# Storing a layer's result per image in 2-KB pieces, and turning it into rows in SBUF, in a four-layer kernel whose order a planner sets

## The chip, the core and the metric

The kernel runs on one core of a Trainium2 chip, everything in float32. The metric is device time in microseconds (us), the median of repeated runs. The engines are PE (matmul; PEld are its weight loads), DVE (vector), ACT (scalar), POOL (GpSimd) and SP, which here only issues DMAs. DMAs are issued by SP, ACT and POOL, and each issuing engine has a DMA queue of its own in the profile: q1 is SP's, q10 ACT's, q0 POOL's.

## What is computed

Four layers on x of shape [8 images, 384 channels, 32, 32]:

```
x = L0(x)   # rmsnorm; Mamba forward and backward: h = dA*h + dBu per channel and 16 states; 3x3 depthwise gate; residual
x = L1(x)   # 1x1, 3x3 depthwise, 1x1; linear attention over the 1024 pixels; layernorm; MLP 384-1536-384, gelu; residuals
x = L2(x)   # one 13x13 depthwise convolution and six smaller ones, each with batch norm, summed
x = L3(x)   # 1x1 + residual, 13x13 depthwise convolution and a scaled identity, gelu
```

Layers 2 and 3 each come down to one 13x13 depthwise convolution with merged taps; in the kernel they are convolution a and convolution b.

## The kernel before

**Layers 0 and 1** (`_layers01`) work image by image. `front(b)` does layer 0's dense part, `scan(b)` the recurrence, `layer1(b)` all of layer 1. Their instructions are woven: while `scan(b)` goes through its 48 steps (12 units of 128 channels and half an image, 4 steps of 4 states each; one `yield` a step), a list of jobs (lines 1195 to 1222) advances `front(b+1)` and `layer1(b-1)` in proportion. `layer1(7)` has no scan beside it and runs alone at the end. A function can be put off by some steps with `defer`, and `tick` calls what is due.

In a scan step ACT computes `da` (L847, the exponentials, four buffers), DVE `du` (L852) and two scans `hs` (L864), POOL multiplies `hs` (L873), and PE adds up states into `acc` (L558). The inputs `dlt`, `vr` and `bct` come by SP's queue (L793, L779). When the backward half of a unit is complete, DVE makes `zr` and POOL stores it to `g_d` (L821). `layer1` begins by loading `g` back (L952, SP) and multiplying it by a weight (`op`, L540), which DVE adds to `xx` (L959).

**Layer 1's result x2** goes to DRAM in `x2_d`, laid out as [channel, image row, RL]: a row holds the 8 images side by side, 32 columns each with 6 zeros before it (`PADW`), RL = 313 in all. `fold` first fills all of `x2_d` with zeros (three DMAs of 5 MB, L901, POOL). `last(h, acc)` adds the MLP's output to `xx` (L1140) and stores it (L1143, POOL), three DMAs for each half image: for every channel 16 pieces of 128 B, one per row of the image.

**Convolution a** (`conv`) takes 8 channels at a time. `load` brings their rows into 32 partitions, one per image row (L301, POOL: 256 pieces of 1252 B); `shift` (L307, DVE) makes three copies that are shifted by one, two and three columns; a group of 4 channels then is 16 matmuls on each of four column groups of PE (L331). The moving operand is 8 images of 32 columns, found by a step of 38 elements in the row. Tap windows come by SP and ACT (L246). The result goes to `y2_d`, the 1x1 of layer 3 (L377) makes `xp_d`, laid out as `x2_d` was, and convolution b reads that.

SBUF tiles of a kind rotate through a fixed number of buffers: `a6` (6 KB a partition) has 7, for `xx`, `g`, `hh`, `dw`, `ln`, `xn` and others. The pool of convolution a reuses the space of the layers before it, each tile waiting for what lay there.

**The order** on each engine is not the program's: `Plan` simulates the program with estimates of every instruction (`Step`, `Engines`) and adds edges that fix the order so found. The engines run in order, so an instruction that waits holds up all that stand behind it on its engine, DMA issues included.

Of the kernel before, what the change touches and what calls it, by code (L numbers as in the profile page):

```python
# [17 lines left out]
P = 128  # L18
C = 384
# [24 lines left out]
AHEAD = 5000  # L44
TP = H * KT
PADW = KS // 2
HIMG = H // 2 * (W + 2)
UL = L + 6
# [21 lines left out]
def tile_layers(  # L70
# [38 lines left out]

    RL = PADW + B * (W + PADW) + 3  # L110
    x2_d = dram.tile([C, H, RL], FP, tag="x2_d", name="x2_d")
    y2_d = dram.tile([C, H, B, W], FP, tag="y2_d", name="y2_d")
# [118 lines left out]

    NB_C = C // NCH
    wins = {}
# [20 lines left out]
    _layers01(tc, nc, B, xv, x2_d, dram, ident, mean_w, eps5, eps6, one, half, minus1, vec, bns, bnt,  # L254
              rs, rsm, inproj_t, xproj_t, dtproj_t, outproj_t, taps1, taps3, taps3b, sel, alog,
# [3 lines left out]
    NQ = C // 4  # L259
    GB = 4  # L260
    with tc.tile_pool(name="cx", bufs=2, reuse_waits="tile") as cxp, tc.tile_pool(
        name="cps", bufs=6, space=PSUM, reuse_waits="tile"
# [12 lines left out]
        for q in range(4):  # L275
            nc.scalar.dma_start(gbias[q * H : (q + 1) * H, :], biasq_d[q, :].partition_broadcast(H))
        def conv(g_d, src_d, tag, put, far):

            xts = {}

            def places(n):

                return [H * ((n % 2 * 2 + e) % NSH) for e in range(NSH)]

            def load(n):
                for m in range(n, min(n + 1 + N_WIN // 2, NB_C)):
                    if (tag, m) not in wins:
                        load_windows(g_d, tag, m, [nc.sync, nc.scalar])  # L290
                if n >= NB_C:
                    return
                at = places(n)
                if "pool" in more and n % 7 >= 4:
                    xt = more["pool"].tile([P, NCH, RL], FP, tag="xu", name=f"xt_{tag}_{n}")
                else:
                    xt = cxp.tile([P, NCH, RL], FP, tag="xt", name=f"xt_{tag}_{n}", bufs=4)
                src = bass.AP(
                    src_d.tensor, src_d[NCH * n, 0, 0].offset, [[RL, H], [H * RL, NCH], [1, RL]],
                )  # L300
                nc.gpsimd.dma_start(xt[at[0] : at[0] + H], src)  # L301
                xts[n] = xt

            def shift(n):
                at, xt = places(n), xts[n]
                for e in (1, 2):
                    nc.vector.tensor_copy(  # L307
                        xt[at[e] : at[e] + e * H, :, 0 : RL - e - (e - 1)],
                        xt[at[0] : at[0] + e * H, :, e : RL - (e - 1)],
                    )  # L310


            for n in range(far):
                load(n)
            shift(0)
            for g in range(NQ):
                n, first = divmod(4 * g, NCH)
                if first == 0:
                    load(n + far)
                    if n + 1 < NB_C:  # L320
                        shift(n + 1)
                    xt, tp = xts.pop(n), wins[tag, n]
                ps = cps.tile([P, HALF], FP, tag="cv", name=f"cv_{tag}_{g}")
                for t in range(KT):
                    for e in range(4):
                        c = first + e
                        row = xt[:, c, NSH * t : NSH * t + B * (W + PADW) - PADW]
                        rhs = bass.AP(
                            row.tensor, row.offset, [row.ap[0], [W + PADW, B], [1, W]]
                        )  # L330
                        nc.tensor.matmul(  # L331
                            ps[H * e : H * (e + 1), 0:BW],
                            tp[:, c, :].rearrange("p (j t) -> p j t", t=KT)[:, :, t], rhs,
                            start=(t == 0), stop=(t == KT - 1), skip_group_check=True,
                        )
                put(g, ps[:, 0:BW])
# [13 lines left out]

        conv(g2_d, x2_d, "a", put2, 2)

# [52 lines left out]
        with tc.tile_pool(name="xu", bufs=3, reuse_waits="tile") as more["pool"]:  # L405
            conv(g3_d, xp_d, "b", put3, 5)


def _layers01(tc, nc, B, xv, x2_d, dram, ident, mean_w, eps5, eps6, one, half, minus1, vec, bns, bnt,
              rs, rsm, inproj_t, xproj_t, dtproj_t, outproj_t, taps1, taps3, taps3b, sel, alog,  # L410
# [11 lines left out]
    with ExitStack() as ctx:  # L422
# [29 lines left out]
        vv = v_d.rearrange("b d (c p) l -> b d p c l", p=P)  # L452
        x2v = x2_d.rearrange("(c p) h r -> c p h r", p=P)

# [442 lines left out]
        def fold():  # L897

            RL = x2_d.shape[2]
            for c in range(NC):  # L900
                fill = nc.gpsimd.dma_start(  # L901
                    x2v[c], zero[:, 0:RL].rearrange("p (o r) -> p o r", o=1).to_broadcast([P, H, RL])
                )

                tc.add_manual_dep(fill.ins, newest[0].ins.name, behind, reason="fill")
                yield 2
            for c in range(NC):
# [36 lines left out]
        def layer1(b):  # L944
# [190 lines left out]
            behind_gelu = []  # L1135

            def last(h, acc):
                for m in range(NC):
                    o = xx[h][:, m, :]
                    nc.vector.scalar_tensor_tensor(  # L1140
                        o, acc[m], vec("mlp_b2", m), o, ALU.add, ALU.add
                    )
                    nc.gpsimd.dma_start(  # L1143
                        x2v[
                            m, :, h * (H // 2) : (h + 1) * (H // 2),
                            PADW + b * (W + PADW) : PADW + b * (W + PADW) + W,
                        ],
                        rows(o),
                    )

# [107 lines left out]
class Step:  # L1258
    def __init__(self, ins, kind_of):
# [16 lines left out]
        elif self.dma:  # L1276
            total = 4 * _count(self.outs[0][1])
            piece = min(4 * _run(self.outs[0][1]), 4 * _run(self.ins[0][1]), 8192)
            self.work = total / piece * (12 + 0.05 * piece) / 16
            self.ns = {"SP": 52.0, "Activation": 330.0, "Pool": 500.0 + min(2048, total / piece) * 0.33}[self.engine]  # L1280
        elif self.engine == "Activation":
# [17 lines left out]
class Engines:  # L1299
    def __init__(self):  # L1300
        self.free = dict.fromkeys(ENGINES, 0.0)
        self.cells, self.mode, self.last = {}, None, 0.0
        self.table, self.port, self.queue = 1, 0.0, 0.0
        self.window, self.busy, self.half = 0, {}, set()

    def clock(self, t):
        now = int(t // CLOCK_NS)
        while self.window < now:
            if self.busy.pop(self.window, 0.0) < BUSY_SHARE * CLOCK_NS:
                self.half.add(self.window + 1)  # L1310
            self.window += 1
# [8 lines left out]
    def put(self, s, ready):  # L1320
        e = s.engine
        if e == "PE":
            t = max(ready, self.free[e])
            if s.mode != self.mode:
                t = max(t, self.last + (95 if self.mode else 0))
                self.cells, self.mode = {}, s.mode
# [24 lines left out]
        if s.table and s.table != self.table:  # L1351
            t, self.table = t + 1290, s.table
        self.free[e] = t + s.ns
# [13 lines left out]
class Plan:  # L1367
    def __init__(self, nc, tiles, traced, spans, bias):
# [30 lines left out]
        self.users = users  # L1399
        areas = {}  # L1400
        for name, t, _, space, size, lo, tag in spans:
            if name in users and kind_of[name] in ("SB", "PSUM"):
                pool = re.sub(r"^.*_(\w+_\d+)$", r"\1", tag)
                areas.setdefault(kind_of[name], []).append((t, lo, lo + max(1, size // P), name, pool))
        for entries in areas.values():
            entries.sort()
            whole = {}
            for _, lo, hi, _, pool in entries:
                a, b = whole.get(pool, (lo, hi))
                whole[pool] = (min(a, lo), max(b, hi))  # L1410
            held, opened = [], {}
            for _, lo, hi, name, pool in entries:
                if pool not in opened:
                    a, b = whole[pool]
                    opened[pool] = sorted({x[2] for x in held if x[0] < b and a < x[1]})
                gates = sorted({x[2] for x in held if x[0] < hi and lo < x[1]}) + opened[pool]
                rest = []
# [5 lines left out]
                held = rest + [(lo, hi, name)]  # L1423
                for g in gates:
                    self.freed.setdefault(g, []).extend(users[name])
# [216 lines left out]
```

## Time and profile before

| | |
|---|---|
| median of 3 runs | 4902.2 us (4898.8 to 4903.2) |
| profiled execution, own time | 4989.3 us |
| its span | 4987.5 us |
| granted PE clock, mean | 0.902 |
| PE busy | 4260.8 us (85%) |
| DVE busy | 3806.8 us (76%) |
| ACT busy | 2712.1 us (54%) |
| POOL busy | 2857.9 us (57%) |
| DMA | 965.3 MB, 194 GB/s |

The stages, from the starts of their instructions: scan 0 begins at 149.8 us, scans 1 to 7 at 657, 1139, 1633, 2136, 2627, 3122 and 3611, each some 490 us; layer 1 of the last image alone from 4046 to 4398; convolution a from 4425 to some 4625; the 1x1 to 4770; convolution b to the end. In the profile's lines `x_d<-xx` is the store of x2, `x_d<-zero` the fill, `x_d<-xr` a store of layer 0, `g_d<-zr` the store of g and `xt_a<-x_d` convolution a's row load (buffer and tensor numbers are left out of names). A line gives the start, the busy time, the engine, the source line, the operation, and in brackets the engine's idle time before it and what ended that.

### The profile page before, as it was taken

How to read it: one execution, taken by the hardware profiler on the slowest of the kernel's cores; microseconds unless marked ns; L12 is line 12 of the kernel's file. 1: busy time of each engine (PE TensorE's matmuls, PEld its weight loads, DVE VectorE, ACT ScalarE, POOL GpSimd, SP SyncE). 2: the span in 40 equal slices, each digit the busy share in tenths (PEclk: the TensorE clock that was granted, in tenths of full speed). 3: DMA queues.
4: the chain of work that ended last, by engine and by line, in shares of the span. 5: the costliest groups of instructions: out<-in, count | busy, mean ns of one | idle time of the engine just before them, and what ended most of it. 6: DMA issues, size and time to landing. Idle time of an engine off the chain costs nothing. (4 is left out here: it accounts for less than half of the span.)

```text
span 4987.5 us, 58465 instructions
## 1 busy us (share of the span) xinstructions
PE 4260.8 (85%) x20128; PEld 1764.7 (35%) x20128; DVE 3806.8 (76%) x3861; ACT 2712.1 (54%) x3786; POOL 2857.9 (57%) x1546
## 2 busy tenths in 40 slices
PE   6665689889989898899888999899988969978888
PEld 2121123333333333333333333333333324457457
DVE  1789989988888898888988998798889840147366
ACT  2546456775587568756875677568645722100212
POOL 1456666666666665666566666565766660024069
PEclk9676699899989998999999989998988978989999
DMA  8985566478747874787478757875763673379788
GB/s 210 277 268 186 191 211 221 158 204 210 225 163 209 209 229 161 202 209 229 167 206 213 227 170 205 214 228 171 171 191 126 165 151 84 63 137 258 224 210 188
DMA packets 543121, 965.29 MB, mean 194 GB/s; under 512 B 56568, under 2 KB 220904, under 8 KB 542824
## 3 DMA queue, kind: packets, MB, share of 16 engines
q1 hardware_dynamic: 401648, 663.89, 45.8%
q0 software_dynamic: 58048, 205.76, 16.5%
q10 hardware_dynamic: 83128, 91.90, 7.0%
q8 instruction: 159, 2.61, 0.2%
q14 instruction: 138, 1.13, 0.1%
HBM read 726.36 MB, written 234.98 MB: 193 GB/s over the span
## 5 line engine op out<-in xcount | busy, mean ns | idle before, releaser
L873 POOL TENSOR_TENSOR hs<-hs,bct 128x1024 f32<-128x1024 f32 x768 | 2260.3, 2944 | 984.3 <-DVE carry L869 517.8
L847 ACT ACTIVATE da<-dlt,neg_a 128x512 f32<-128x512 f32 x1536 | 1026.7, 714 | 697.6 <-DVE hs L864 621.2
L852 DVE TENSOR_TENSOR du<-vr,bct 128x1024 f32<-128x1024 f32 x768 | 1052.9, 1371 | 45.3 <-DMA vr<-v_d 27.6
L864 DVE TENSOR_TENSOR_SCAN hs<-da,carry,du 128x512 f32<-128x512 f32 x768 | 946.7, 1267 | 96.1 <-PE acc L558 61.0
L864 DVE TENSOR_TENSOR_SCAN hs<-da,du 128x512 f32<-128x512 f32 x768 | 904.1, 1209 | 65.8 <-ACT da L847 19.9
L558 PE MATMUL acc<-hs,selt 128*32 128x512 f32 x2304 | 610.6, 672 | 102.5 <-POOL hs L873 102.5
L540 PE MATMUL mf<-ln,w 128*128 128x512 f32 x1152 | 552.1, 621 | 48.3 <-DMA w<-w_d 18.0
L1173 PE MATMUL mo<-hm,w 128*128 128x512 f32 x1152 | 526.9, 596 | 0.0
L553 PE MATMUL acc<-hs,selt 128*32 128x512 f32 x768 | 444.9, 676 | 89.1 <-POOL hs L873 63.0
L847 ACT ACT_TABLE_LOAD x282 | 361.8, 1283 | 10.3 <-DMA bct<-bc_d 2.0
L540 PEld LDWEIGHTS mf<-ln,w 128*128 128x128 f32 x1152 | 217.3, 197 | 360.0 <-issue 284.8
L1173 PEld LDWEIGHTS mo<-hm,w 128*128 128x128 f32 x1152 | 215.0, 190 | 291.9 <-issue 282.6
L540 PE MATMUL in<-xn,win 128*128 128x512 f32 x576 | 281.8, 626 | 9.9 <-ACT uz L669 5.2
L331 PE MATMUL cv_a<-xt_a,tp_a 128*32 128x256 f32 x3072 | 181.9, 388 | 48.8 <-DMA xt_a<-x_d 27.8
L1143 POOL DMA_DIRECT2D x_d<-xx x48 | 56.6, 1181 | 276.8 <-DVE xx L1140 275.9
L540 PE MATMUL op<-g,wo 128*128 128x512 f32 x288 | 149.9, 671 | 75.8 <-DMA g<-g_d 75.1
L331 PE MATMUL cv_b<-xt_b,tp_b 128*32 128x256 f32 x3072 | 180.2, 392 | 27.6 <-DVE xt_b L307 15.5
L558 PE MATMUL dw<-dw_i,t3b 96*32 96x512 f32 x1056 | 194.1, 641 | 6.5 <-DMA dw_i<-h_d 6.1
L553 PEld LDWEIGHTS acc<-hs,selt 128*32 128x32 f32 x768 | 63.4, 115 | 365.2 <-issue 241.7
L307 DVE COPY xt_b<-xt_b 32x2496 f32<-32x2496 f32 (+1 forms) x96 | 151.8, 1581 | 49.8 <-DMA xt_b<-xp_d 47.3
L331 PEld LDWEIGHTS cv_a<-xt_a,tp_a 128*32 128x32 f32 x3072 | 157.1, 138 | 73.9 <-DVE xt_a L307 28.7
L558 PEld LDWEIGHTS acc<-hs,selt 128*32 128x32 f32 x2304 | 91.9, 114 | 235.5 <-POOL hs L873 166.2
(196 smaller groups left out, 5891.2 us busy)
## 6 DMA issues: line engine op xcount, KB each, us to landing
dlt<-dl_d SPq DMA_DIRECT2D x384, 256.0 KB, 4.2
vr<-v_d SPq DMA_DIRECT2D x384, 256.0 KB, 5.0
bct<-bc_d SPq DMA_DIRECT2D x256, 256.0 KB, 5.4
ut<-u_d SPq DMA_DIRECT2D x192, 257.5 KB, 4.9
lc_i<-xn_d SPq DMA_DIRECT2D x192, 228.8 KB, 4.9
dw_i<-h_d SPq DMA_DIRECT2D x192, 228.8 KB, 6.2
w<-w_d SPq DMA_DIRECT2D x64, 576.0 KB, 5.2
w<-in_w SPq DMA_DIRECT2D x64, 576.0 KB, 6.4
```

The source lines that it names most:

```text
L307: nc.vector.tensor_copy(xt[at[e] : at[e] + e * H, :, 0 : RL - e - (e - 1)], xt[at[0] : at[0] + e * H, :, e : RL - (e - 1)],)
L331: nc.tensor.matmul(ps[H * e : H * (e + 1), 0:BW], tp[:, c, :].rearrange("p (j t) -> p j t", t=KT)[:, :, t], rhs, start=(t == 0), stop=(t = ...
L540: product = nc.tensor.matmul(ps, w[:, k, m * P : (m + 1) * P], rhs[k] if isinstance(rhs, list) else rhs[:, k, :], start=(k == 0), stop=(k ...
L553: first = product()
L558: tc.keep_in_program_order(product())
L847: nc.scalar.activation(da[:, bass.ts(j, HALF)], dlt[:, bass.ts(j, HALF)], AF.Exp, scale=neg_a[:, g, r : r + 1],)
L852: nc.vector.tensor_mul(pairs(du), pairs(vt), bct[r][:, 0:1, :].to_broadcast([P, 2, HALF]),)
L864: nc.vector.tensor_tensor_scan(t[:, s][:, way], da[:, s][:, way], du[:, s][:, way], k_c if second else 0.0, ALU.mult, ALU.add,)
L873: made.append(nc.gpsimd.tensor_mul(pairs(t), pairs(t), bct[r][:, 1:2, :].to_broadcast([P, 2, HALF])))
L1143: nc.gpsimd.dma_start(x2v[m, :, h * (H // 2) : (h + 1) * (H // 2), PADW + b * (W + PADW) : PADW + b * (W + PADW) + W,], rows(o),)
L1173: nc.tensor.matmul(acc[m], wb[:, f, m * P : (m + 1) * P], hm, start=(i == 0 and f == 0), stop=(i == FF // C - 1 and f == NC - 1),)
```

## The change

x2 is stored in its natural order in a new tensor `x2i_d` [image, channel, pixel], so that a piece is 512 pixels of a channel, 2 KB. For images 0 to 6 a new step `turn` reads it back with one partition per image row and stores whole padded rows into a new `x2_d`; there is no fill any more. Image 7 isn't turned: convolution a reads it from `x2i_d` directly. `load` for convolution a becomes one POOL load (images 0 to 6), two memsets of pads and one SP load (image 7), and a row of the tile now holds images outermost and 8 channels inside. Convolution b is as before. The planner's estimates are changed, so the order of all engines is new.

```diff
-    x2_d = dram.tile([C, H, RL], FP, tag="x2_d", name="x2_d")
+    x2_d = dram.tile([NB_C, H, B - 1, NCH, WP], FP, tag="x2_d", name="x2_d")
+    x2i_d = dram.tile([B, C, L], FP, tag="x2i_d", name="x2i_d")
...
+                if last_d is not None:
+                    own = flat(xt)[at[0] : at[0] + H]
+                    near = (B - 1) * NCH * WP
+                    nc.gpsimd.dma_start(own[:, 0:near], src_d[n].rearrange("h b c w -> h (b c w)"))
+                    end = own[:, near : near + (NCH + 1) * WP].rearrange("p (c w) -> p c w", w=WP)
+                    nc.gpsimd.memset(end[:, :, 0:PADW], 0.0)
+                    nc.gpsimd.memset(own[:, XF - 3 : XF], 0.0)
+                    nc.sync.dma_start(
+                        end[:, 0:NCH, PADW:WP],
+                        last_d[NCH * n : NCH * (n + 1)].rearrange("c (h w) -> h c w", w=W),
+                    )
...
-            for c in range(NC):
-                fill = nc.gpsimd.dma_start(
-                    x2v[c], zero[:, 0:RL].rearrange("p (o r) -> p o r", o=1).to_broadcast([P, H, RL])
-                )
...
+            def turn(b, k):
+                t = a6(f"turn_{b}_{k}").rearrange("p c n -> p (c n)")[:, 0 : RC * WP]
+                t = t.rearrange("p (c w) -> p c w", w=WP)
+                nc.gpsimd.memset(t[:, :, 0:PADW], 0.0)
+                for q in range(4):
+                    src = bass.AP(
+                        x2i_d.tensor, x2i_d[b, q * QC + k * RC, 0].offset, [[W, H], [L, RC], [1, W]]
+                    )
+                    nc.sync.dma_start(t[q * H : (q + 1) * H, :, PADW:WP], src)
+                for q in range(4):
+                    n = (q * QC + k * RC) // NCH
+                    nc.scalar.dma_start(
+                        x2_d[n : n + RC // NCH, :, b].rearrange("n h c w -> h n (c w)"),
+                        t[q * H : (q + 1) * H].rearrange("p (n c) w -> p n (c w)", c=NCH),
+                    )
...
-                    nc.gpsimd.dma_start(
-                        x2v[
-                            m, :, h * (H // 2) : (h + 1) * (H // 2),
-                            PADW + b * (W + PADW) : PADW + b * (W + PADW) + W,
-                        ],
-                        rows(o),
-                    )
+                    nc.gpsimd.dma_start(x2v[b][:, m, bass.ts(h, HALF)], o)
+                if h and b < B - 1:
+                    for k in range(QC // RC):
+                        defer(2 * k + 1, partial(turn, b, k))
...
-CLOCK_NS, BUSY_SHARE = 3413.0, 0.8
-LANES = 8
+CLOCK_NS, STAYS, RETURNS = 3413.0, 0.41, 0.83
+LANES, LANDS = 8, 1500
...
+                need = RETURNS if self.window in self.half else STAYS
+                if self.busy.pop(self.window, 0.0) < need * CLOCK_NS:
...
-                t = max(t, self.last + (95 if self.mode else 0))
+                t = max(t, self.last + (0 if not self.mode else 195 if self.mode[1] == "32" else 95))
...
-            self.queue = max(t + 1300, self.queue) + s.work
-            return t, self.queue + 700
+            own = self.queues.get(e, 0.0)
+            if s.small:
+                self.queues[e] = max(t + 1300, own, self.queue - s.work / 2) + s.work
+                self.queue = max(t + 1300, self.queue) + 0.6 * s.work
+            else:
+                self.queues[e] = max(t + 1300, self.queue, own) + s.work
+                self.queue = max(t + 1300, self.queue) + s.work
+            return t, self.queues[e] + LANDS
```

Here C is 384, H and W 32, L 1024, NCH 8, PADW 6, WP 38, QC 96 and RC 32, so `turn` runs three times per image (k = 0, 1, 2). What the planner treats as small DMA writes are those of pieces under 512 B and over 1500 pieces; a switch to another table on ACT is taken at 1400 instead of 1290 ns; and the rule by which tiles of a pool wait for the pools before it is written anew.

More of the change, by code (lines that the diff above doesn't have):

```diff
@@ L45 @@
 TP = H * KT
+NB_C = C // NCH
 PADW = KS // 2
+WP = W + PADW
+QC = C // 4
+RC = 32
 HIMG = H // 2 * (W + 2)
@@ L230, in kernels @@
         yield 1
-    NB_C = C // NCH
     wins = {}
@@ L252, in windows @@
             yield
-    _layers01(tc, nc, B, xv, x2_d, dram, ident, mean_w, eps5, eps6, one, half, minus1, vec, bns, bnt,
+    _layers01(tc, nc, B, xv, x2_d, x2i_d, dram, ident, mean_w, eps5, eps6, one, half, minus1, vec, bns, bnt,
               rs, rsm, inproj_t, xproj_t, dtproj_t, outproj_t, taps1, taps3, taps3b, sel, alog,
@@ L260, in tile_layers @@
     GB = 4
+    XF = B * NCH * WP + WP - W + 3
     with tc.tile_pool(name="cx", bufs=2, reuse_waits="tile") as cxp, tc.tile_pool(
@@ L276, in tile_layers, with conv, flat @@
             nc.scalar.dma_start(gbias[q * H : (q + 1) * H, :], biasq_d[q, :].partition_broadcast(H))
-        def conv(g_d, src_d, tag, put, far):
+        def conv(g_d, src_d, last_d, tag, put, far):
             xts = {}
+            def flat(xt):
+                return xt.rearrange("p c r -> p (c r)")
             def places(n):
@@ L297, in load @@
                     xt = cxp.tile([P, NCH, RL], FP, tag="xt", name=f"xt_{tag}_{n}", bufs=4)
+                if last_d is not None:
[9 more added lines that the diff above has]
+                    )
+                    xts[n] = xt
+                    return
                 src = bass.AP(
@@ L305, in shift @@
                 at, xt = places(n), xts[n]
+                if last_d is not None:
+                    xt = flat(xt)
+                    for e in (1, 2):
+                        nc.vector.tensor_copy(
+                            xt[at[e] : at[e] + e * H, 0 : XF - e - (e - 1)],
+                            xt[at[0] : at[0] + e * H, e : XF - (e - 1)],
+                        )
+                    return
                 for e in (1, 2):
@@ L326, in conv @@
                         c = first + e
-                        row = xt[:, c, NSH * t : NSH * t + B * (W + PADW) - PADW]
-                        rhs = bass.AP(
-                            row.tensor, row.offset, [row.ap[0], [W + PADW, B], [1, W]]
-                        )
+                        if last_d is not None:
+                            row = flat(xt)[:, c * WP + NSH * t : XF]
+                            step = NCH * WP
+                        else:
+                            row = xt[:, c, NSH * t : NSH * t + B * WP - PADW]
+                            step = WP
+                        rhs = bass.AP(row.tensor, row.offset, [row.ap[0], [step, B], [1, W]])
                         nc.tensor.matmul(
@@ L349, in put2 @@
                 nc.gpsimd.dma_start(y2v[g - GB + 1 : g + 1].rearrange("g p n -> p g n"), hold["t"])
-        conv(g2_d, x2_d, "a", put2, 2)
+        conv(g2_d, x2_d, x2i_d[B - 1], "a", put2, 2)
         pbias = cwp.tile([P, NC, 1], FP, tag="pbias", name="pbias")
@@ L405, in tile_layers, with _layers01 @@
         with tc.tile_pool(name="xu", bufs=3, reuse_waits="tile") as more["pool"]:
-            conv(g3_d, xp_d, "b", put3, 5)
-def _layers01(tc, nc, B, xv, x2_d, dram, ident, mean_w, eps5, eps6, one, half, minus1, vec, bns, bnt,
+            conv(g3_d, xp_d, None, "b", put3, 5)
+def _layers01(tc, nc, B, xv, x2_d, x2i_d, dram, ident, mean_w, eps5, eps6, one, half, minus1, vec, bns, bnt,
               rs, rsm, inproj_t, xproj_t, dtproj_t, outproj_t, taps1, taps3, taps3b, sel, alog,
@@ L452, in _layers01 @@
         vv = v_d.rearrange("b d (c p) l -> b d p c l", p=P)
-        x2v = x2_d.rearrange("(c p) h r -> c p h r", p=P)
+        x2v = chunks(x2i_d)
         def const(ap, shape, tag):
@@ L897, in fold @@
         def fold():
-            RL = x2_d.shape[2]
-            for c in range(NC):
-                fill = nc.gpsimd.dma_start(
-                    x2v[c], zero[:, 0:RL].rearrange("p (o r) -> p o r", o=1).to_broadcast([P, H, RL])
-                )
-                tc.add_manual_dep(fill.ins, newest[0].ins.name, behind, reason="fill")
-                yield 2
             for c in range(NC):
@@ L1135, in layer1 @@
             behind_gelu = []
+            def turn(b, k):
[12 more added lines that the diff above has]
+                        t[q * H : (q + 1) * H].rearrange("p (n c) w -> p n (c w)", c=NCH),
+                    )
             def last(h, acc):
@@ L1142, in last @@
                     )
-                    nc.gpsimd.dma_start(
-                        x2v[
-                            m, :, h * (H // 2) : (h + 1) * (H // 2),
-                            PADW + b * (W + PADW) : PADW + b * (W + PADW) + W,
-                        ],
-                        rows(o),
-                    )
+                    nc.gpsimd.dma_start(x2v[b][:, m, bass.ts(h, HALF)], o)
+                if h and b < B - 1:
+                    for k in range(QC // RC):
+                        defer(2 * k + 1, partial(turn, b, k))
             for h in range(2):
@@ L1279, in __init__ @@
             self.work = total / piece * (12 + 0.05 * piece) / 16
+            self.small = piece < 512 and total / piece > 1500 and kind_of.get(self.outs[0][0]) != "SB"
+            if self.small:
+                self.work = total / piece * 60 / 16
             self.ns = {"SP": 52.0, "Activation": 330.0, "Pool": 500.0 + min(2048, total / piece) * 0.33}[self.engine]
@@ L1302, in __init__ @@
         self.cells, self.mode, self.last = {}, None, 0.0
-        self.table, self.port, self.queue = 1, 0.0, 0.0
+        self.table, self.port, self.queue, self.queues = 1, 0.0, 0.0, {}
         self.window, self.busy, self.half = 0, {}, set()
@@ L1308, in clock @@
         while self.window < now:
-            if self.busy.pop(self.window, 0.0) < BUSY_SHARE * CLOCK_NS:
+            need = RETURNS if self.window in self.half else STAYS
+            if self.busy.pop(self.window, 0.0) < need * CLOCK_NS:
                 self.half.add(self.window + 1)
@@ L1342, in put @@
             self.free[e] = t + s.ns
-            self.queue = max(t + 1300, self.queue) + s.work
-            return t, self.queue + 700
+            own = self.queues.get(e, 0.0)
+            if s.small:
+                self.queues[e] = max(t + 1300, own, self.queue - s.work / 2) + s.work
+                self.queue = max(t + 1300, self.queue) + 0.6 * s.work
+            else:
+                self.queues[e] = max(t + 1300, self.queue, own) + s.work
+                self.queue = max(t + 1300, self.queue) + s.work
+            return t, self.queues[e] + LANDS
         if s.lock:
@@ L1351, in put @@
         if s.table and s.table != self.table:
-            t, self.table = t + 1290, s.table
+            t, self.table = t + 1400, s.table
         self.free[e] = t + s.ns
@@ L1399, in __init__ @@
         self.users = users
-        areas = {}
+        areas, turns = {}, {}
         for name, t, _, space, size, lo, tag in spans:
@@ L1404, in __init__ @@
                 areas.setdefault(kind_of[name], []).append((t, lo, lo + max(1, size // P), name, pool))
+                first, final = turns.get(pool, (n, 0))
+                turns[pool] = (min(first, users[name][0]), max(final, users[name][-1]))
         for entries in areas.values():
             entries.sort()
[L1407 to L1411, printed above, removed]
+            members = {}
+            for e in entries:
+                members.setdefault(e[4], []).append(e[3])
+            held = []
             for _, lo, hi, name, pool in entries:
[L1413 to L1416, printed above, removed]
+                gates = {x[2] for x in held if x[0] < hi and lo < x[1]}
+                for other, names in members.items():
+                    if turns[other][1] < turns[pool][0]:
+                        gates.update(names)
                 rest = []
@@ L1423, in __init__ @@
                 held = rest + [(lo, hi, name)]
-                for g in gates:
+                for g in sorted(gates):
                     self.freed.setdefault(g, []).extend(users[name])
```

## The prediction

> **What bounds the kernel now.** I read the page first (span 4987.5 us), then the windows of each image's scan, then the waits, then timelines at the three places where this change acts. The eight scans of layer 0 (one per image, with the previous image's layer 1 and the next image's front woven in) take most of the span. A middle one, its last 28 us before the next image settles, and a hole in the first scan:
>
> ```profile
> 2136.00:2624.00 488.00, 440.62 (x1685) 164.51 (x1682) 421.19 (x419) 331.77 (x452) 303.73 (x146) 0.94 0.70 202
> 1632.20:1660.00 27.80, 23.46 (x81) 8.59 (x79) 26.25 (x31) 9.50 (x15) 17.57 (x14) 0.99 1.02 127
> 250.00:276.00 26.00, 1.92 (x4) 0.18 (x4) 11.64 (x14) 0.02 (x1) 5.20 (x3) 0.50 1.00 269
> ```
>
> Columns: stretch, its length, busy us (instructions) of PE, weight loads, DVE, ACT, POOL, then granted clock, DMA share, GB/s. In 488 us PE works 441 and DVE 421: both are near their limit, DMA (0.70) is not. But right after a scan's end (second line) DMA is full at only 127 GB/s, and in the first scan (third line) everything stands but DMA. What waits on that:
>
> ```profile
> PE op L540 <- DMA g<-g_d: 75.1, 7, 15.0
> POOL hh L578 <- DMA x_d<-xx: 44.2, 5, 12.7
> ```
>
> Seven waits of PE for the load of g (total, times, longest), five of POOL for x2 stores. The timeline after scan 2 shows how:
>
> ```profile
> 1632.20 3.52 POOL L1143 DMA_DIRECT2D x_d<-xx  x3
> 1642.82 0.61 POOL L821 DMA_DIRECT2D g_d<-zr  x1
> 1658.30 0.47 POOL L578 MEMSET hh<- 128x48 f32 x4 [5.45 <-DMA x_d<-xx]
> 1659.70 0.38 SPq L952 DMA_DIRECT2D g<-g_d  x1
> 1665.27 10.08 PE L540 MATMUL op<-g,wo 128*128 128x512 f32 x18 [9.61 <-DMA g<-g_d]
> 1670.23 0.75 DVE L959 SCALAR_TENSOR_TENSOR xx<-op,rsm,xx 128x512 f32<-128x512 f32 x1 [8.92 <-PE op L540]
> ```
>
> POOL issues three x2 stores in 128-B pieces; the small store of g follows on POOL's queue and lands 16.9 us after its issue began. After scan 0, where no x2 store is ahead of it, it took 3.1 us. So the g load starts at 1659.7, PE idles 9.6 us and DVE 8.9 us behind it. The last transition, from layer 1 to convolution a:
>
> ```profile
> 4395.71 2.47 DVE L1140 SCALAR_TENSOR_TENSOR xx<-mo,pk,xx 128x512 f32<-128x512 f32 x3 [59.29 <-PE mo L1173]
> 4400.48 4.89 POOL L271 MEMSET xo<- 128x1878 f32 x3
> 4408.49 1.20 POOL L301 DMA_DIRECT2D xt_a<-x_d  x2 [3.13 <-DMA x_d<-xx]
> 4420.75 8.86 DVE L307 COPY xt_a<-xt_a 32x2496 f32<-32x2496 f32 x6 [22.57 <-DMA xt_a<-x_d]
> 4425.21 15.09 PE L331 MATMUL cv_a<-xt_a,tp_a 128*32 128x256 f32 x220 [27.82 <-DMA xt_a<-x_d]
> ```
>
> PE stands 27.8 us: store landing 11 us, row load 12.3 us, two shifts. Median landings of the stores concerned:
>
> ```profile
> x_d<-zero POOLq DMA_DIRECT2D x3, 5008.0 KB, 45.5
> x_d<-xx POOLq DMA_DIRECT2D x48, 256.0 KB, 16.9
> x_d<-xr POOLq DMA_DIRECT2D x48, 256.0 KB, 5.1
> ```
>
> The third, a store of layer 0 with the same 256 KB in 2-KB pieces, is the form that the x2 store gets.
>
> **The fill (removed).** Three zero fills of 5 MB leave POOL's queue at 170, 190 and 219 us, 45.5 us each. A store behind them (c_d, 237 us) lands 33.2 us after its issue; POOL waits 24.1 us for it, SP and ACT stand behind, and DVE idles 14.8 us at 276.8 (plus 2.6 and 1.2 us on loads). Without the fill that store should land in about 3 us, like its twin at 308 us. Scan 0 is DVE's (462 busy of 506 us), so this idle time is span. Ends: 5 us (another wait comes up) and 19 us. I take **15 us**.
>
> **The x2 store in 2-KB pieces.** POOL's issue falls from 1.18 to 0.58 us (L688): 48 x 0.6 = 29 us of a POOL that is busy 304 of 488, off the path. What counts is landing, 5 instead of 17 us. After scans 1 to 6 DVE's wait at L959 is 12.6, 9.5, 13.2, 11.4, 9.7 and 5.2 us, together 61.6; after scan 0, without x2 stores ahead, it is 2.9. If g lands as there, 61.6 - 6 x 2.9 = 44 us go. Left next is that 2.9 us. The POOL waits of 44 us (L578) mostly overlap those stalls; I count nothing for them. The 15.0-us wait for g after scan 7 has no x2 store in front and stays.
>
> **The turn (added, 7 images x 3).** Each k adds a memset, 4 loads (SP) of 1024 pieces of 128 B, and 4 stores (ACT) of 128 pieces of 1216 B.
> - POOL: 21 memsets of 192 columns; the nearest row (L578, 48 columns) is 0.21 us, so 0.2 to 0.9 each, under POOL's idle time: 0. Uncovered, at most 19 us.
> - SP: 84 issues of 0.5 to 0.7 us, as L793. If the first load is placed before its x2 store has landed, SP stands, and the scan's dlt, vr and bct loads with it; they run ahead by 6 buffers. ACT: 84 issues of 0.33 us, 28 us of an engine 332/488 busy. Its stores wait for the turn's loads, and the exponentials (L847) queue behind; four da tiles cover them, some 4 x 3.7 us of DVE work (two scans of 1.2 and du of 1.2 us). Price 0 while the wait is under that.
> - DMA time. Between 4405 and 4435 us the trace's DMA packets of the x2 stores (32 pieces of 128 B each) took 1067 ns on average, 33 ns a piece. Reads of 128 B into SBUF occur in the trace only as 512 start-up packets: median 13 ns, mean 18. The skill's page "DMA: Bandwidth & Descriptors", section Specifications, speaks against the change: below 512 B an engine does read-modify-write[...]. By that rule the pieces merely move: 12,288 per image x 33 / 16 = 25 us, as before, on SP's queue, and the stalls remain. By the trace's reads it is 12,288 x 13 to 18 / 16 = 10 to 14 us, plus row stores (55 ns, the 1276-B packets) 1536 x 55 / 16 = 5 us. I take the trace's reads: they go the same way (HBM to SBUF), while the 33 ns were measured on writes into HBM. Of the two I lean to the 18 ns, since the turn's pieces lie scattered.
> - Where it lies: in program order 1, 3 and 5 scan steps of some 10 us (490 us / 48) after the last x2 store. The g load comes back some 15 to 25 us after it, so on SP's queue it can stand behind the four loads of k = 0, 0.8 to 1.1 us of DMA each: 0 to 4.4 us. I take 1.5 us for each of six: **-9 us**; ends 0 and -44 (by the rule above, all of the gain).
> - Three more tiles in the 7 a6 buffers may delay hh or xn tiles: in the range only.
>
> Together 44 - 9 = **35 us**.
>
> **Transition and convolution a.** New chain: last DVE result 4396.8 to 4398.2, issue 0.6, landing 3 to 5 (4402), direct load of 256 pieces 3 to 4 (4406), two shifts 3 us, matmul near 4410 instead of 4425.2. If POOL runs the three xo memsets (4.9 us) before the row load, 4412. That is 13 to 18 us; **15 us**. Within convolution a PE has 166 busy of 187 us: row loads carry 272 KB in 8.5-KB runs and 32 KB in 128-B pieces instead of 313 KB; at the rows above 0.7 to 1.9 + 0.2 to 0.5 us of DMA per tile against 2: even. 96 POOL memsets (0.1 to 0.2 us, POOL 72 of 187 busy), SP's 48 loads, the moving rows' step of 304 instead of 38 elements (no row shows it; runs stay 32 long): 0, ends -8 and +5.
>
> **The other order.** The planner's estimates of clock, mode switch, landing and pool gates change, so every queue is reordered. PE idles some 47 us and DVE 67 of a scan's 488, of which the above touches about 10. No row says what the new order gains: between -40 and +100 us over seven scans; I take 0, since waits of the same engines must still be filled.
>
> **Sum.** The profiled execution took 4989.3 us (span 4987.5). 15 + 35 + 15 = 65 gives 4924. The median of the runs is 4902.2, 0.9825 of it: 65 x 0.9825 = 64, so **4838 us**.
>
> **Rivals.**
> 1. The turn takes the stalls' place: its reads cost 33 ns, hold SP's queue, g still comes late. For: DMA is already full there. Against: only SP's ring is shared, and POOL's g store is then free. Leaves 15 + 15 = 30, x 0.98: 4873.
> 2. The order fills idle time too: 10 us more in each of seven scans; 4838 - 69 = 4769. For: 47 us idle; against: no row.
> 3. Slower: ACT stands at the turn's stores. In the crowded stretch loads landed in 15.3 us (dlt, 1645); four in a row plus this could outlast the 15 us of da cover. It decides at 65 / 21 = 3 us uncovered per turn; at 6 us, 126 - 65 = 61 us more, x 0.98: 4962. Against: ACT waits 71 us per scan for DVE, and the planner places the stores after a later landing (1500 instead of 700 ns).
> 4. No change: the boundary stalls return as waits for hs or a6 buffers, and only part of the rest comes: about 4900.
>
> Chances: forecast 0.46 (4815 to 4860), rival 1 0.22, rival 2 0.20, no change 0.05, slower 0.07. A measurement of this kernel can tell about 0.2% from no change. Faster 0.88, same 0.05, slower 0.07. The range 4762 to 4890 leaves out the lower third of rival 2, no change and slower.
>
> **What would show it.** Right: the g store lands in 3 to 6 us after scans 1 to 6 and L959 waits under 5 us; no 15-us DVE gap near 277 us; PE idle before convolution a 10 to 15 us; x2 landing near 5 us. Wrong: turn loads landing over 10 us with g behind them; ACT's exponentials waiting for turn loads; DVE busy per scan unchanged and the idle time grown elsewhere.

## The result, and the profile after

The changed kernel took 4826.4 us (median of 4 runs, 4812.3 to 4835.0) against 4902.7 us for the kernel before beside it: ratio 0.984, 95% interval 0.981 to 0.987, that is 76 us faster (64 were predicted). The kernel before is not equally fast in every set of runs (a set is one group of runs on one chip, with the kernel before among them): it gave 4902.7 here and 4960.2, 4926.4 and 4927.4 us beside the experiments, the first two of these three on the same chip, while the changed one gave 4826.4, 4832.3 and 4835.4. So the ratio itself ranges from 0.975 to 0.984, and the experiments are judged by ratios within their own set and by stage lengths; where the two disagree, both are given. The profiled execution of after took 4812.3 us (span 4810.4), the fastest of its runs; that of before was 87 us over its median. Their difference, 177 us, is therefore not the change's worth.

The windows of the same four places, with the columns as before (stretch, length, busy us of PE, weight loads, DVE, ACT, POOL, clock, DMA share, GB/s): a middle scan, the 28 us behind the end of scan 2, the former hole in scan 0, and convolution a.

```profile
2044.80:2512.50 467.70, 437.10 (x1698) 164.47 (x1697) 432.75 (x424) 335.89 (x455) 310.56 (x152) 0.97 0.71 222
1575.50:1603.30 27.80, 23.90 (x83) 8.17 (x83) 26.57 (x31) 11.20 (x18) 19.48 (x11) 0.94 0.97 258
250.00:276.00 26.00, 16.90 (x90) 4.87 (x82) 25.87 (x34) 9.41 (x15) 15.11 (x6) 0.79 0.87 234
4226.50:4454.50 228.00, 183.35 (x3073) 158.33 (x3073) 151.81 (x141) 17.50 (x47) 87.47 (x155) 0.97 1.07 222
```

The middle scan has become 20 us shorter with nearly the same work of PE (437 us, 441 before); what went is mostly idle time. After the scan's end DMA is nearly as full as before, but moves 258 instead of 127 GB/s. The hole is gone (DVE 25.9 of 26 us). Convolution a, 202.9 us before, is now 228. Its row of before:

```profile
4425.20:4628.10 202.90, 181.91 (x3073) 157.23 (x3073) 154.27 (x141) 17.54 (x47) 76.05 (x67) 0.99 1.07 246
```

PE's work is the same within 2 us; DMA is full in both, but carries less. PE's wait for g, in after's list of waits (total, times, longest):

```profile
PE op L573 <- DMA g<-g_d: 23.3, 3, 17.0
```

75.1 us in seven waits became 23.3 in three, and 17.0 of that is the wait after scan 7, which was expected to stay. DVE's waits for `op` from scan 1 to the end of scan 7, before and after:

```profile
DVE xx L959 <- PE op L540: 61.6, 12, 12.3
```

```profile
DVE xx L984 <- PE op L573: 10.1, 11, 2.6
```

The timeline after scan 2, to be laid beside that of before:

```profile
1575.48 1.66 POOL L1185 DMA_DIRECT2D x2i_d<-xx  x3
1584.75 0.58 POOL L854 DMA_DIRECT2D g_d<-zr  x1
...
1579.90 9.62 SPq L1171 DMA_DIRECT2D turn<-x2i_d  x8
1594.78 0.67 SPq L977 DMA_DIRECT2D g<-g_d  x1
...
1604.55 2.08 PE L573 MATMUL op<-g,wo 128*128 128x512 f32 x2
```

The g store lands 3.6 us after its issue (16.9 before). The g load starts only 6 us after that landing, behind eight loads of the turn and others on SP's queue, yet PE has no gap: the new order gives PE and DVE other work until 1604. After scans 1 to 6 the g store lands in 3.2 to 6.5 us. The transition to convolution a:

```profile
4208.27 2.47 DVE L1182 SCALAR_TENSOR_TENSOR xx<-mo,pk,xx 128x512 f32<-128x512 f32 x3 [54.18 <-PE mo L1212]
...
4213.71 4.86 POOL L276 MEMSET xo<- 128x1878 f32 x3 [2.14 <-DMA xt_a<-x2i_d]
4218.53 0.52 POOL L310 DMA_DIRECT2D xt_a<-x_d  x1
...
4222.08 8.70 DVE L331 COPY xt_a<-xt_a 32x2440 f32<-32x2440 f32 x6 [11.34 <-DMA xt_a<-x_d]
...
4226.51 4.08 PE L364 MATMUL cv_a<-xt_a,tp_a 128*32 128x256 f32 x36 [16.57 <-DVE xt_a L331]
```

PE stands 16.6 us (27.8 before). What ends it is not image 7's direct read but the row load of images 0 to 6, which stands on POOL behind the three memsets of 4.9 us. Median landings:

```profile
x_d<-turn ACTq DMA_DIRECT2D x84, 152.0 KB, 3.6
g_d<-zr POOLq DMA_DIRECT2D x48, 256.0 KB, 2.9
x2i_d<-xx POOLq DMA_DIRECT2D x48, 256.0 KB, 4.6
turn<-x2i_d SPq DMA_DIRECT2D x84, 128.0 KB, 4.9
```

At the median the x2 store lands in 4.6 us, where it took 16.9.

### The profile page after: what moved, and what is told of

Same layout as the page of the kernel before. It is cut to its first block, busy times and chain, and to the rows that moved or that the text cites. A ratio compares the mean times of both kernels' runs of the same rounds, so it can differ in the third digit from the quotient of the medians.

```text
span 4810.4 us, 59001 instructions
## 1 busy us (share of the span) xinstructions
PE 4201.2 (87%) x20128; PEld 1741.9 (36%) x20128; DVE 3834.4 (80%) x3861; ACT 2717.4 (56%) x3788; POOL 2860.2 (59%) x1660
## 4 chain that ended last, share of the span: by engine, by line
PE 45%; DVE 20%; issue 14%; DMA 12%; ACT 6%; POOL 3%; SPq 0%; ACTq 0%; DVEq 0%; POOLq 0%
DVE hs L897 11%; DVE du L885 5%; PE mo L1212 5%; PE mf L573 5%; PE in L573 4%; PE acc L586 4%; DMA tp_a<-g_d 3%; PE kv_kp L1037 2%; PE c L573 2%; PE pj L573 2%; PE kv_vt L1037 2%; ACT da L880 2%; PE dw L591 2%; PE h L573 2%; DMA tp_b<-g_d 2%
## 5 line engine op out<-in xcount | busy, mean ns | idle before, releaser
L885 DVE TENSOR_TENSOR du<-vr,bct 128x1024 f32<-128x1024 f32 x768 | 1068.8, 1392 | 31.3 <-DMA vr<-v_d 15.1
L573 PE MATMUL mf<-ln,w 128*128 128x512 f32 x1152 | 544.3, 612 | 29.0 <-DVE xn L684 15.4
L364 PE MATMUL cv_b<-xt_b,tp_b 128*32 128x256 f32 x3072 | 179.8, 390 | 27.2 <-DVE xt_b L337 15.4
L1185 POOL DMA_DIRECT2D x2i_d<-xx x48 | 26.5, 553 | 285.4 <-DVE xx L1182 284.2
L331 DVE COPY xt_a<-xt_a 32x2440 f32<-32x2440 f32 (+1 forms) x96 | 137.4, 1431 | 46.6 <-DMA xt_a<-x2i_d 20.3
```

Source lines behind the costliest of these rows:

```text
L331: nc.vector.tensor_copy(xt[at[e] : at[e] + e * H, 0 : XF - e - (e - 1)], xt[at[0] : at[0] + e * H, e : XF - (e - 1)],)
L364: nc.tensor.matmul(ps[H * e : H * (e + 1), 0:BW], tp[:, c, :].rearrange("p (j t) -> p j t", t=KT)[:, :, t], rhs, start=(t == 0), stop=(t = ...
L573: product = nc.tensor.matmul(ps, w[:, k, m * P : (m + 1) * P], rhs[k] if isinstance(rhs, list) else rhs[:, k, :], start=(k == 0), stop=(k ...
L885: nc.vector.tensor_mul(pairs(du), pairs(vt), bct[r][:, 0:1, :].to_broadcast([P, 2, HALF]),)
```

## The experiments

Two questions: which part of the change makes the scans shorter, and why convolution a lost 25 us. Theory 1 is the prediction's: the gain is the boundary stalls behind g and comes with the layout. Its rivals: the new order does it; or slow small pieces delay much more than g. The planner orders every kernel anew, so no edit changes one thing alone. Three profiles of the unaltered changed kernel (4810, 4837, 4828 us) show how closely stages repeat: scans 1 to 7 take 3218, 3229 and 3233 us together, convolution a 228.0, 231.2 and 223.9.

**The two kernels again.** No edit. For the kernel before:

> The kernel before, unchanged, as a control. The profile of before (4989 us) lies 87 us over the median of its runs, that of the changed kernel on the fastest of its runs. If that profile was a slow execution, this one comes near 4905 us in the profile too, with the same boundary stalls (store of g landing in 16 to 18 us) and shorter idle times elsewhere. If profiling itself costs this kernel 87 us, it is near 4989 us again.

Measured: 4963.0 us, ratio 1.0003 (0.9992 to 1.0014). Its profiled execution took 4970 us, inside the range of its other runs (4946 to 4971): profiling does not cost 87 us, and the whole set is slower. For the changed kernel:

> The changed kernel, unchanged, on the chip of e1 to e3: 4826 us plus or minus 12. Both theories say the same; it is what the others are compared with.

Measured: 4832.3 us, ratio 0.9746 (0.9724 to 0.9768), 128 us faster in this set of runs.

**The order alone.** Layout, stores and fill of before, with the changed planner:

```diff
-CLOCK_NS, BUSY_SHARE = 3413.0, 0.8
+CLOCK_NS, STAYS, RETURNS = 3413.0, 0.41, 0.83
...
-            return t, self.queue + 700
+            return t, self.queues[e] + LANDS
```

> The layout of before, with the changed planner. Theory 1 (the layout's DMAs: store landing, fill, transition): the order alone gives little, 4880 to 4905 us; the g store still lands in 16 us behind the x2 stores and PE waits for g after scans 1 to 6. Theory 2 (the order): most of the 76 us is here, 4825 to 4850 us, and the scans are shorter by some 8 us each.

Measured: 4864.6 us, ratio 0.9804 (0.9788 to 0.9821): 96 us faster, where the whole change gave 128 in this set. Its timeline after scan 2:

```profile
1600.70 3.60 POOL L1143 DMA_DIRECT2D x_d<-xx  x3
1610.47 0.61 POOL L821 DMA_DIRECT2D g_d<-zr  x1 [0.25 <-DVE zr L820]
...
1630.49 0.55 SPq L952 DMA_DIRECT2D g<-g_d  x1
...
1638.83 7.89 PE L540 MATMUL op<-g,wo 128*128 128x512 f32 x18
```

The g store is as late as ever (17.2 us), but the last line has no bracket: PE does not wait. The new order has `op` later and other matmuls before it; which of the changed estimates does this was not tried. The stall can be cured without making the store faster.

**The layout alone.** The changed layout with all the old estimates of the planner (clock, mode switch, landing, small pieces, table switch); only the new rule for the pools stays. Two of the lines:

```diff
-CLOCK_NS, STAYS, RETURNS = 3413.0, 0.41, 0.83
-LANES, LANDS = 8, 1500
+CLOCK_NS, BUSY_SHARE = 3413.0, 0.8
+LANES = 8
```

> The changed layout, with the old estimates of the planner (clock, mode switch, landing, table switch); only the new rule for a pool's tiles is kept, without which this layout's order is not sound. Theory 1: 4825 to 4850 us, nearly all of the gain; g lands in 3 to 6 us. Theory 2: 4870 to 4900 us.

Measured: 4874.7 us, ratio 0.983 (0.9813 to 0.9847), 86 us faster. Alone the parts gain 96 and 86 us, together 128: they overlap by 53 us. In the profile of before of this set DVE's waits for `op` in scans 1 to 7 are 56 us; the order alone leaves 14 and the layout alone 5. So some 42 us of the overlap are these waits, which either part cures; the rest was not traced. In scans 1 to 7 the layout alone gains 111 us (3374 to 3263), far over the 35 predicted.

**The store alone.** The order-alone kernel with x2 stored in 2-KB pieces to a tensor of its own; no turn, and convolution a reads zeros in place of x2:

```diff
-                    nc.gpsimd.dma_start(
-                        x2v[
-                            m, :, h * (H // 2) : (h + 1) * (H // 2),
-                            PADW + b * (W + PADW) : PADW + b * (W + PADW) + W,
-                        ],
-                        rows(o),
-                    )
+                    nc.gpsimd.dma_start(x2iv[b][:, m, bass.ts(h, HALF)], o)
```

> The layout of before with the changed planner, and the x2 store alone changed to 2-KB pieces into a tensor of its own; no turn, and convolution a reads the zero-filled rows, so layers 0 and 1 are left out of its input. Compared with the order alone (4865 us): theory 1 (the 128-B writes slow everything that lands beside them and hold POOL) expects the scans 6 to 10 us shorter each, 4790 to 4825 us in all with a shorter transition. If the boundary stall was all that the writes cost, and the new order already hides it, the scans stay as in the order alone, near 4850 us (the transition alone).

Measured: 4774.6 us, ratio 0.9689 (0.9666 to 0.9712); scans 1 to 7 take 3207 us against 3287 for the order alone, though PE did not wait for g after scans 1 to 6 in that kernel. How much this is depends on the measure, since the two ran in different sets: 80 us by the stage and 90 by the medians, but 57 by the ratios (0.9804 to 0.9689). Whether the order-alone kernel varies from set to set as the kernel before does was not measured. And the order moved again: 82% of DVE's instructions follow in the same sequence, so a part may be the order's. Where the time was: waits of the order-alone kernel, then of this one.

```profile
DVE xx L993 <- PE c L540: 139.5, 26, 75.7
DVE hs L864 <- PE acc L558: 90.5, 31, 7.1
ACT da L847 <- DMA dlt<-dl_d: 45.0, 9, 10.7
PE in L540 <- DMA win<-in_inproj_t: 26.5, 8, 11.4
```

```profile
DVE xx L995 <- PE c L542: 114.6, 18, 79.3
DVE hs L866 <- PE acc L560: 52.5, 16, 8.9
ACT da L849 <- DMA dlt<-dl_d: 21.2, 10, 5.8
PE in L542 <- DMA win<-in_inproj_t: 8.9, 1, 8.9
```

DVE's two waits fall by 25 and 38 us (they are counted over the whole span), and loads of the scan that have nothing to do with x2 (dlt, win) come sooner. The small writes had slowed what shares the DMA engines: summed over the packets of scans 1 to 7, the engines worked 2253 us each in the first kernel and 2056 in the second. Of the difference 114 us are on POOL's queue, which carries x2; but SP's queue (293,887 and 293,871 packets) also fell from 1741 to 1688 us and ACT's (30,784 in both) from 178 to 150, for the same transfers.

**The x2 store on SP's queue.** The order-alone kernel, 128-B pieces kept, issued by SP instead of POOL:

```diff
-                    nc.gpsimd.dma_start(
+                    nc.sync.dma_start(
```

> The kernel before's layout with the changed planner, its 128-byte store of x2 issued on SP's queue instead of POOL's. Queue theory (the taps' store lands late because it stands behind the x2 stores in POOL's queue): with the x2 stores gone from that queue the taps' store lands in 2.3 to 5 us after scans 1 to 6 instead of 15 to 18. Congestion theory (small pieces make every queue slow): it lands in 10 us or more. For the time: SP's queue carries dlt and the other loads of the scan, which then stand behind a store of 2048 small pieces: by the queue theory these land later and the time is 4870 to 4930 against 4865 for the order alone; by congestion alone 4855 to 4875.

Measured: 4861.5 us, ratio 0.987 (0.9855 to 0.9885).

```profile
g_d<-zr POOLq DMA_DIRECT2D x48, 256.0 KB, 5.0
x_d<-xx SPq DMA_DIRECT2D x48, 256.0 KB, 12.5
```

With POOL's queue free of x2, the g store still lands in 10.4, 12.1, 12.1, 12.3, 8.4 and 6.5 us after scans 1 to 6, 10.3 on average, against 15.4 behind the x2 stores and 2.3 in the store-alone kernel. Of the 13 us too many, some 5 were the place in the queue and 8 the crowd in the engines, as far as differently ordered kernels can be compared. Neither theory was right alone. The time does not decide: it is 3 us under the order alone by the medians, as congestion had it, and 33 us over it by the ratios, as the queue theory had it.

**The fill put back.** Three fills of the same size into a tensor that nobody reads:

```diff
+                fill = nc.gpsimd.dma_start(
+                    fv[c], zero[:, 0:RL].rearrange("p (o r) -> p o r", o=1).to_broadcast([P, H, RL])
+                )
```

> The changed kernel with the three 5-MB zero fills put back, into a tensor that nobody reads. If the fill cost 15 us in the first scan, as predicted: 4832 + 15 = 4847 us, with scan 0 near 510 us. If the new order hides it: under 5 us more, scan 0 at 495 to 500 us.

Measured: 4823.3 us, ratio 0.9788 (0.9765 to 0.9812; the sets differ, so the stage decides). Scan 0 takes 495.8 us against 492.4 to 495.2 without the fill. The store of c_d behind the fills still lands late (23.9 us), but DVE's wait at this place is 6.1 instead of 14.8 us. Scan 1 begins at 635 us here and at 645 to 652 without the fill. At the new order the fill costs next to nothing.

**The turn twice.** Each turn is made a second time into a spare tensor:

```diff
+                turned(b, k, x2e_d)
+                turned(b, k, x2_d)
```

> Every turn is made twice, the first time into a tensor that nobody reads: 84 more loads of 1024 pieces of 128 B, 84 more stores. Theory 1 (a turn is hidden, 13 to 18 ns per piece): at most 15 us more, 4832 to 4847. Rival 1 of the prediction (33 ns per piece, in the way of g and the scan's loads): 40 us or more on top, 4875 or above.

Measured: 4928.1 us, ratio 1.0005 (0.9994 to 1.0016): all of the gain is lost. Theory 1's 15 us were far exceeded. Scans 1 to 7 take 3326 us, 93 to 108 more than with one turn, 4.4 to 5.1 us per added turn. Its waits, then those of after:

```profile
ACT da L881 <- DMA dlt<-dl_d: 93.7, 16, 12.5
DVE du L886 <- DMA vr<-v_d: 49.1, 13, 16.9
```

```profile
ACT da L880 <- DMA dlt<-dl_d: 22.8, 12, 5.0
DVE du L885 <- DMA vr<-v_d: 15.1, 1, 15.1
```

ACT and DVE wait for loads of the scan that are issued on SP's queue, where the turn's loads stand too; the turn's packets stay at 15.9 ns, so the cost is not rival 1's 33 ns per piece. This is rival 3's size of cost, reached at twice the turns, though through SP's queue more than through ACT's.

**The turn's loads in long pieces.** 4-KB pieces instead of 128 B; the rows hold the values in another order:

```diff
-                        x2i_d.tensor, x2i_d[b, q * QC + k * RC, 0].offset, [[W, H], [L, RC], [1, W]]
+                        x2i_d.tensor, x2i_d[b, q * QC + k * RC, 0].offset, [[L, RC], [1, L]]
```

> The changed kernel with the turn's loads in pieces of 4 KB instead of 128 bytes (1536 packets fewer to 48 per load; the rows it makes hold the values in another order). Theory 1 (the turn costs by its standing in SP's and POOL's queues and by its buffers, and its 98304 small reads at 16 ns are 98 us of each engine in 4810, hidden mostly): scans 1 to 7 lose 0 to 8 us, the time falls by 0 to 10 us. Rival (the small reads are the 22 us that the scans of the changed kernel are longer than those of the kernel that only stores in 2-KB pieces): the scans fall by 15 to 22 us and the time with them.

With the unaltered kernel in the same set:

> The changed kernel, unaltered, as the base for the three beside it: 4826 to 4832 us, conv a 228 to 231 us and the 1x1 stage 126 us, as in its two earlier profiles. Both theories expect the same.

Measured: 4800.4 us, ratio 0.9749 (0.9729 to 0.977), against 4835.4 us, ratio 0.9819 (0.98 to 0.9838). Scans 1 to 7 take 3206 us instead of 3233, about what they take in the store-alone kernel with no turn at all (3207). So the turn costs 27 us in the scans by this pair, 11 to 27 with the other two profiles of the changed kernel, and by its small pieces: theory 1 missed. Their packets are as short as predicted (15.4 ns on average in those scans), but 84,992 of them are 82 us of each of the 16 engines, the long ones 38. The planner keeps most of its order here, not all (84% of DVE's instructions and 70% of SP's follow in the same sequence), so a part of the 27 us may be the order's.

**No direct read of image 7.** All eight places of a row are stored by the turn (image 6's rows a second time in the place of image 7), and convolution a loads only rows:

```diff
-                    near = (B - 1) * NCH * WP
+                    near = B * NCH * WP
...
-                    nc.sync.dma_start(
-                        end[:, 0:NCH, PADW:WP],
-                        last_d[NCH * n : NCH * (n + 1)].rearrange("c (h w) -> h c w", w=W),
-                    )
```

> The changed kernel without the direct read: the new x2 layout has a place for 8 images, image 7's place is filled with image 6's rows by 12 further row stores after its last turn, and convolution a's load is one load of 9728-B runs; so image 7's result is left out of layer 2. Theory A (convolution a is at the DMA engines' limit and the 128-B direct reads are its new 25 us): convolution a falls from 231 to 205 to 212 us and the time by some 20 us, to about 4810. Theory B (the 28 us come from the reordered tap windows or the image-outermost rows on PE): convolution a stays at 225 to 232 us.

Measured: 4806.3 us, ratio 0.9754 (0.9734 to 0.9774).

```profile
4239.40:4441.90 202.50, 178.40 (x3073) 158.00 (x3073) 152.01 (x141) 17.50 (x47) 75.34 (x111) 0.99 1.07 246
```

Convolution a is back at 202.5 us, with the same steps of the moving operand and rows of the same form. The direct reads, with the memset that goes with them, are the 25 us. (The time does not show it as well: 20 to 29 us under the changed kernel by the medians, but the same ratio as its 0.9746 in another set.)

**Late windows of convolution b.** They run inside convolution a in both kernels; from the ninth on they are put behind the 1x1's loads:

```diff
-                load_windows(g3_d, "b", t, [nc.scalar, nc.sync])
+                if t < 8:
+                    load_windows(g3_d, "b", t, [nc.scalar, nc.sync])
+                else:
+                    load_windows(g3_d, "b", t, [nc.sync], got)
```

> The changed kernel with the tap windows of convolution b from the ninth on (12 of 20) put on SP's queue behind the 1x1's load of the same step, so that they no longer run inside convolution a. Theory A (convolution a is held by the 16 DMA engines: 1.07 of their time in the profile of after, 48 thousand 512-byte packets at 45 ns are 136 us per engine of its 228): 12 windows of 1024 packets at 45 ns are 35 us of each engine; taken out of convolution a it ends 20 to 35 us earlier, and the 1x1 stage, which has its DMA engines busy for 0.63 of 127 us, takes them in for 0 to 8 us: 10 to 35 us faster than the changed kernel. Rival (convolution a is slow because the rows of the last image come late, 20 us of DVE's waits, and PE waits for DVE's shifts, not for the DMA engines): convolution a stays at 222 to 231 us, and the 1x1 or convolution b loses 5 to 15 us by windows that come late.

Measured: 4828.3 us, ratio 0.9796 (0.9774 to 0.9817), not to be told from the 0.9819 of its set.

```profile
4255.40:4474.70 219.30, 182.78 (x3073) 158.56 (x3074) 151.90 (x141) 17.55 (x48) 86.97 (x155) 0.97 0.95 204
4483.80:4610.20 126.40, 126.37 (x288) 55.50 (x288) 35.77 (x94) 36.53 (x47) 11.26 (x15) 0.98 0.85 249
```

DMA is no longer full in convolution a (0.95), the 1x1 took the windows in for nothing, and convolution a still lasts 219 us (224 in the unaltered kernel of its set). Room in the DMA engines was worth 5 of the 25 us, no more than the 7 us by which the three profiles of the unaltered kernel differ, and not 20 to 35: theory A, in the form put here, falls. Waits in convolution a of the changed kernel:

```profile
PE cv_a L364 <- DMA tp_a<-g_d: 10.8, 9, 2.1
PE cv_a L364 <- DMA tp_b<-g_d: 8.4, 4, 4.4
DVE xt_a L331 <- DMA xt_a<-x2i_d: 20.3, 10, 3.6
DVE xt_a L331 <- DMA xt_a<-x_d: 8.2, 3, 4.9
```

Before the change DVE waits 13.7 us for rows in convolution a, without direct reads 15.0, in the changed kernel 28.5 and here 19.4, which follows the stage's length (203, 202, 228, 219 us). PE itself waits for no DVE shift but one (3.3 us); it waits 19.2 us for what the profile takes to be tap windows (11.3 here), which it does not do before the change or without direct reads. The windows land no later than before (7.3 to 7.4 us at the median, 8.7 to 8.9 before), so the profile may put a wait for image 7's rows down to them. Late rows are thus the likelier cause, but not a shown one. Whether they are late by SP's queue, where each stands behind tap windows, or by the shape of the transfer, stays open.

## Why the prediction was right, and where it was not

The time and its direction were right; of the steps, the boundary was, and five terms were mis-sized, some against each other. By stages of the two kernels that ran again in one set (before, then after): scans 1 to 7 3374 to 3229 (-145), scan 0 with the time ahead of it 652 to 652, the transition 25.8 to 16.7 (-9), convolution a 205.0 to 231.2 (+26), the gap behind it 15.9 to 10.8 (-5), the rest +3: together -130. By the medians of that set the layout alone gave 86 us where 65 were forecast for it, and the order added 42 where 0 was forecast.

- **Boundary stalls, 44 us: right in mechanism and near in size.** Landings of 3.2 to 6.5 us against 3 to 6 forecast; the DVE waits fell from 61.6 to 10.1 us, and in the set above from 56 to 12. But the new order cures the same stalls without the faster store (order alone).
- **The x2 store: the failed step is counting only the stalls behind g.** Between equal planners, where PE had no wait for g left after scans 1 to 6, the store still was worth 57 to 90 us by the measure taken, with whatever the order that comes with it adds. The small writes also slowed dlt and win, and DVE's waits for PE shrank without them. The window at 1.02 DMA share and only 127 GB/s pointed to it; the prediction read it for the g store alone.
- **The turn, 9 us: mis-sized.** The piece price was right: the 98,304 reads of 128 B took 13 ns at the median and 15.9 ns at the mean, inside 13 to 18, and not the 33 ns per piece of the x2 writes (a mean over the 192 packets of the last three stores, which start between 4400 and 4415 us, not between 4405 and 4435). The Trainium skill's rule (page "DMA: Bandwidth & Descriptors", Specifications: under 512 B an engine does read-modify-write; the row names no direction) does not show as a price per read here. The row stores took 69 ns a packet where 55 was used. What failed is taking most of those reads as hidden: they cost 11 to 27 us, over the forecast's 9 and under rival 1's 44.
- **"The other order", 0 us: mis-sized.** Alone it gained 96 us, the upper end of the stated -40 to +100, and beside the layout 42. The reason given for 0, that waits of the same engines must still be filled, was wrong: other work was there to fill them.
- **The fill, 15 us: wrong beside the new order.** The hole at 277 us is gone and scan 0 is 8 us shorter (502.3 to 494.7), but putting the fill back does not bring the hole back, and the time ahead of scan 0 grew by as much.
- **Transition, 15 us: 9 to 11.** The 4.9 us of memsets ahead of the row load, named as a possibility, came true.
- **Convolution a, "even": wrong by 25 us.** Only the DMA time of a tile was compared; what a second load on SP's queue adds to the chain of each tile, with only two loaded ahead, was put at nothing.
- **A term that was missing: PE's own busy time.** In scans 1 to 7 it fell from 3035 to 2991 us for the same matmuls, at a granted clock of 0.931 before and 0.944 after; PE's idle time fell from 340 to 238. What of the 43 us shortened the stage was not tested.

Rival 2, the order filling idle time, was therefore largely right, rivals 1 and 3 in part: the small reads do cost, and at twice the turns all is lost. Part of the agreement in size is luck: 145 us in the scans where 35 were forecast, 15 for the fill that are not there, 26 lost in convolution a, and a kernel before that in the first set ran 24 to 58 us faster than later. Why it varies so and the changed kernel does not is open. None of the kernels that compute the whole beats the changed one by more than its interval.

## What to carry to other kernels

A store in small pieces can cost everything that shares the DMA engines while it runs, not only what waits for it: look for a full DMA share at low GB/s. A stall behind a late transfer has two cures, a faster transfer or other work in the gap, and their gains do not add. When a load is made cheaper in bytes but gains a second part, follow the chain of one tile and the depth of prefetch too, not only the engines' sum.

## What was not expected of the hardware

Small pieces cost by direction, and in the tail. On the same queue, SP's, 98,304 pieces of 128 B took 27.4 ns on average when they were written to DRAM (the store on SP's queue) and 15.9 when they were read into SBUF (the changed kernel). At the median both took 13 ns; but 4.6% of the writes took over 100 ns, and 8 of all the reads. The writes held other queues' stores back (the g store landed in 10.3 us with its own queue free of them, 2.3 without them); with the reads on SP's queue it landed in 4.3 us on average. In convolution a, long runs into 32 partitions were no cheaper by the byte: the 8.5-KB packets took 612 ns on average and the 5-KB packets of the order-alone kernel 332 ns.
